# Attention in phases of two slots, with two chunk chains and streamed keys

## The chip, the cores and the metric

The kernel runs on one core of a Trainium2 chip. The metric is the device time of one execution in microseconds (us). Engines are named as in the profile: PE multiplies matrices (PEld is its weight load), DVE is the vector engine, ACT the scalar engine, POOL GpSimd, SP the queue that issues most DMAs. SBUF is the memory that all of them read; PSUM is what PE writes[...].

## The reference, cut to what matters

The network has a Mamba layer and then attention over 2 images of 4096 positions and 256 channels, 8 heads of 32. The change is in the attention alone:

```python
x = x + _L0_conv_ref(_gn(x), ...)            # Mamba layer, unchanged
x = x + _L1_conv_ref(_gn(x), qkv_w, qkv_b, 8)

def _L1_conv_ref(x, qkv_w, qkv_b, num_heads):
    qkv = jnp.einsum('bchw,oc->bohw', x, qkv_w) + qkv_b[None, :, None, None]
    q, k, v = ...                            # (b, 8, 32, 4096) each
    attn_logits = jnp.einsum('bhci,bhcj->bhij', q, k) * scale
    attn_weights = jax.nn.softmax(attn_logits, axis=-1)
    out = jnp.einsum('bhij,bhcj->bhci', attn_weights, v)
    return out.reshape(b, c, h, w)
```

## The kernel before

The Mamba stage comes first and takes the span to about 1995 us. Attention works through image 0, then prepares image 1 (projections of q, k and v, each stored to DRAM and loaded again), then works through image 1. A planner orders the Mamba stage; attention is written out by hand, and each engine runs its instructions in that order.

An image is 2 groups of 4 heads by 8 query tiles of 512 positions, so 16 tiles. Each tile runs over 32 slots, and a slot is 128 keys for 512 queries and 4 heads. A slot needs four logits products on PE (L1162, 128 x 512 each, one PSUM bank each), the exponential on ACT (L1175), four values products (L1199, one per head, accumulated in the bank po), and the sum of the exponentials over all keys, which is the denominator of the softmax.

A slot has two halves, of two heads and so two banks. The six banks of the tile s hold three halves, and a phase is three halves: `sizes` and PHASES (L1144 to L1146) give 20 phases of three halves and two of two in each tile. In `run` (L1314) iteration k has the exponentials of phase k, then the values of phase k-1, then one step of the finishing work of the tile before for each slot (`side.run`), then the logits of phase k+1. In a phase of three halves the values of one slot are whole, 512 columns, and those of another half are 256 columns (`width`, L1193).

The denominators are summed on two engines. The exponentials of heads 0 and 1 go to a buffer `chunk`, which holds four slots side by side; when it is full DVE sums it with one TENSOR_REDUCE into the first place of the next of two buffers (L1184, ten times a tile), and `place` (L1178) says where a slot goes. Heads 2 and 3 go to a tile e. POOL adds both to acc_p (L1239), but in the 15 slots of SHARED it adds one head (L1237), and DVE adds the other to acc_2 in PSUM (L1236). `finish` (L1241) copies po, adds the partial sums (L1249, L1250), sums over the 128 rows on PE with a matrix of ones (L1257), takes reciprocals, multiplies (POOL, L1267), adds bias and residual and stores. `end` (L1276) does it for the last tile.

Keys of a group stay in SBUF: `load_keys` (L1104) loads eight tiles of 1 MB, in two DMAs each, once per group, during the last query tile of the group before.

Of the kernel before, what the change touches and what calls it, by code (L numbers as in the profile page):

```python
# [11 lines left out]
F32 = mybir.dt.float32  # L12
# [17 lines left out]
def group_norm_scales(nc, small, psum_tile, stats, gmat, eps_t, out):  # L30
# [9 lines left out]
    yield  # L40
    ps = psum_tile()
    for k in range(KC):
        nc.tensor.matmul(ps[:, k : k + 1], lhsT=gmat, rhs=mv[k][:, 0:1], start=True, stop=True)
    for k in range(KC):
        nc.vector.tensor_copy(out[k][:, 0:1], ps[:, k : k + 1])

# [5 lines left out]
    yield 4  # L52
    ps = psum_tile()
    for k in range(KC):
        nc.tensor.matmul(ps[:, k : k + 1], lhsT=gmat, rhs=e[k][:, 1:2], start=True, stop=True)
    yield
# [5 lines left out]
class Slots:  # L62
# [10 lines left out]
    def run(self):  # L73
        for entry in list(self.waiting):
            if entry[0] <= self.now:
                try:
                    entry[0] = self.now + (next(entry[1]) or 1)
                except StopIteration:
                    self.waiting.remove(entry)
        self.now += 1  # L80

# [887 lines left out]
def attention(ctx, tc, stats, consts, w, outs, scratch, range_t):  # L969
# [14 lines left out]
    SCALE = 1.0 / math.sqrt(D)  # L984

    p2 = ctx.enter_context(tc.tile_pool(name="l1p2", bufs=2))
    wp = ctx.enter_context(tc.tile_pool(name="l1w", bufs=1))
    ps_s = ctx.enter_context(tc.tile_pool(name="l1pss", bufs=3, space=PSUM))
# [10 lines left out]
    kp = ctx.enter_context(tc.tile_pool(name="l1k", bufs=NT))  # L999
    ep = ctx.enter_context(tc.tile_pool(name="l1e", bufs=5))  # L1000
    ec = ctx.enter_context(tc.tile_pool(name="l1c", bufs=2))
    p1 = ctx.enter_context(tc.tile_pool(name="l1p1", bufs=1))
    p3 = ctx.enter_context(tc.tile_pool(name="l1p3", bufs=2))
    kq = ctx.enter_context(tc.tile_pool(name="l1kq", bufs=1))
# [4 lines left out]
    def s_tile():  # L1009
        return ps_s.tile([P, 2, T], F32, name="s", tag="s")  # L1010

    def chunk():

        return ec.tile([P, 2, 2, T, 2], F32, name="chunk")

    FIRST = 3
    xn = {}  # L1020

    def load_x(t):
# [7 lines left out]
        else:  # L1030
            xn[t] = ep.tile([P, KC, T], F32, name="e")
# [8 lines left out]
    def project(t, i):  # L1040


        pm = s_tile()
        for m in range(KC):
            for c in range(KC):
                nc.tensor.matmul(  # L1046
# [6 lines left out]
        halves = chunk().rearrange("p q h t k -> p q (h t k)").rearrange("p q (m t) -> p q m t", t=T)  # L1053
        for m in range(KC):
            bias = b_qkv[:, i * KC + m : i * KC + m + 1]
            nc.scalar.activation(halves[:, 0, m, :].bitcast(F32R), pm[:, m, :], AF.Identity, bias=bias)
            nc.vector.scalar_tensor_tensor(
                halves[:, 1, m, :].bitcast(F32R), pm[:, m, :], bias, halves[:, 0, m, :], ALU.add, ALU.subtract
            )
            nc.sync.dma_start(scratch.qk[KG + m, i, t].rearrange("s c h t -> (c h) s t"), halves[:, :, m, :])  # L1060

    def project_values(t):
        pm = s_tile()
        flat = pm.rearrange("p a t -> p (a t)")
        for j in range(T // P):
            for c in range(KC):
                nc.tensor.matmul(
# [6 lines left out]
        nc.scalar.copy(v[:, bass.ts(t, T // P), :].rearrange("p s c -> p (s c)"), flat)  # L1074

    def prepare(image):

        for t in range(NT):
# [15 lines left out]
            if 0 < t <= FIRST:  # L1094
                image.load_keys(0, t - 1)
        for t in range(FIRST, NT):
            image.load_keys(0, t)

    def image(b):
# [4 lines left out]
        def load_keys(g, t, queue=nc.sync):  # L1104


            k = keys[g, t] = (kq if g and t == 0 else kp).tile([P, 4, T], F32R, name="k")
            load_stack(queue, k, scratch.qk[b * KG + g, 1, t], 1)
# [7 lines left out]
        def load_prepared():  # L1116
# [6 lines left out]
            load_keys(0, 0, nc.scalar)  # L1123
            load_values(0, 0, nc.scalar)
            for t in range(1, NT):
                load_keys(0, t)
                load_values(0, t)
# [16 lines left out]
        sizes = [3] * ((2 * NC - 4) // 3) + [2, 2]  # L1144
        bounds = [0, *itertools.accumulate(sizes * (KG * NT))]
        PHASES = [range(*ends) for ends in zip(bounds, bounds[1:])]  # L1146
        SHARED = [c for c in range(8, NC) if c % 8 in (0, 2, 4, 5, 6)]
        todo = {}
        tiles = {}

        def logits(s, half):
            if s >= S:
                return
            i, c = divmod(s, NC)
            kt, kj = divmod(c * P, T)
            if half == 0:
                todo[s] = Slot()
                todo[s].s, todo[s].e = [], []
            ps = s_tile()
            for j in range(2):  # L1160
                h = 2 * half + j
                nc.tensor.matmul(  # L1162
                    ps[:, j, :], lhsT=keys[i // NT, kt][:, h, kj : kj + P], rhs=queries[i][:, h, :], start=True, stop=True
                )
            todo[s].s.append(ps)

        def exponentials(s, half):
            if half == 0 and s % NC < NC - 1:
                k = place(s % NC)
                first = s % NC == 0 or k == 1 and s % NC > 1  # L1170
                todo[s].chunk = (todo.pop("chunk", None) or chunk()) if first else todo[s - 1].chunk
                e = todo[s].chunk[:, k // 2, :, :, k % 2]
            else:
                e = ep.tile([P, 2, T], F32, name="e")
            nc.scalar.activation(e, todo[s].s[half], AF.Exp, scale=SCALE)  # L1175
            todo[s].e.append(e)

        def place(c):  # L1178

            return c if c < 4 else 1 + (c - 4) % 3  # L1180

        def sum_chunk(s, out):
            terms = todo[s].chunk.rearrange("p q h t k -> p (h t) q k")
            nc.vector.tensor_reduce(out, terms, AX.XY, ALU.add)  # L1184

        def values(first, end):

            u = first
            while u < end:
                s, half = divmod(u, 2)  # L1190
                i, c = divmod(s, NC)
                g = i // NT
                width = 2 if half == 0 and u + 1 < end else 1  # L1193
                cols = slice(half * T // 2, (half + width) * T // 2)
                u += width
                if c == 0 and half == 0:
# [363 lines left out]
```

## Time and profile before

| what | us |
|---|---|
| median of 3 runs (lowest, highest) | 4287.68 (4287.12, 4287.88) |
| profiled execution, its time | 4289.86 |
| its span, first to last instruction | 4288.1 |
| PE, DVE, ACT, POOL busy in the span | 4119.0, 3855.6, 3729.2, 3751.9 |
| logits products L1162, 4096 of them, busy | 1155.0 |
| values products L1199, busy (into chunk rows, into e rows) | 1057.0, 1020.5 |
| exponentials L1175, to chunk and to e, mean of one | 1.126, 1.028 |
| chunk sums L1184 on DVE, mean of one | 4.409 |
| POOL additions L1239 and L1237, mean of one | 2.432, 1.297 |

The mean granted clock of PE is 0.984 over the span and 1.00 in attention. "Busy" is the time in which an engine executes at least one instruction; products overlap, so a busy PE is not a PE at its peak. A group's row has its line, engine and operation, the tiles it writes and reads, shapes and count, then busy time and the mean of one in ns, then the idle time before it and what ended that. The chain of waits follows the program back from its last instruction, at each step to what released it.

### The profile page before, as it was taken

Reading aid. Unit: us, or ns where it says so; the run is one execution under the profiler, and the core shown is the slowest. Engines: PE = TensorE matmul, PEld = TensorE weight load, DVE = VectorE, ACT = ScalarE, POOL = GpSimd, SP = SyncE. Lnnn points to the kernel's source line nnn. Section 1 sums busy time; section 2 is a strip of 40 time slices with the busy share of each in tenths; the row PEclk is TensorE's granted clock in tenths of the full one; section 3 lists DMA queues with packets and bytes.
Section 4 is the critical chain, followed back from the end, with each engine's and each line's share of the span. In section 5 each row is a group of like instructions: output and inputs, shape, how many; then the busy total and the mean of one; then the engine's idle time right before and its main releaser. Section 6 shows DMA issues by size and latency. Waiting matters only on the chain.

```text
span 4288.1 us, 58982 instructions
## 1 busy us (share of the span) xinstructions
PE 4119.0 (96%) x21176; PEld 1802.7 (42%) x21176; DVE 3855.6 (90%) x3304; ACT 3729.2 (87%) x4983; POOL 3751.9 (87%) x1913
## 2 busy tenths in 40 slices
PE   6799999999999999988999999999999999999998
PEld 2233333333333343333444444444454444444443
DVE  6899999999999999994988989899849889898998
ACT  5789898999788888874999999999859999999997
POOL 3999999999899999994888988889728989888897
PEclk8899999999999999999999999999999999999999
DMA  6334333344444444447101040110181110401100
GB/s 212 105 114 130 113 113 126 129 133 133 150 144 163 154 141 142 142 167 168 34 24 28 18 106 18 28 30 21 40 262 46 40 28 18 106 18 28 30 21 9
DMA packets 172302, 389.58 MB, mean 91 GB/s; under 512 B 23392, under 2 KB 49760, under 8 KB 163808
## 3 DMA queue, kind: packets, MB, share of 16 engines
q1 hardware_dynamic: 171120, 383.37, 29.4%
q8 instruction: 168, 2.75, 0.3%
q10 hardware_dynamic: 880, 2.36, 0.3%
q14 instruction: 134, 1.10, 0.1%
HBM read 292.33 MB, written 93.32 MB: 90 GB/s over the span
## 4 chain that ended last, share of the span: by engine, by line
PE 82%; DVE 10%; ACT 3%; issue 2%; DMA 1%; POOL 1%; SPq 0%; DVEq 0%; POOLq 0%; ACTq 0%
PE s L1162 25%; PE po L1199 24%; PE mm L448 16%; DVE h L869 6%; PE y L901 4%; PE mm L688 4%; PE bn L448 2%; PE mm L647 2%; DVE bn L860 1%; PE s L1046 1%; PE y L899 1%; PE mm L684 1%; PE sums_ps L1257 1%; ACT da L853 1%; ACT L248 1%
## 5 line engine op out<-in xcount | busy, mean ns | idle before, releaser
L1184 DVE TENSOR_REDUCE chunk<-chunk 128x1024 f32<-128x4096 f32 x288 | 1269.9, 4409 | 169.5 <-ACT chunk L1175 168.2
L1239 POOL TENSOR_TENSOR acc_p<-acc_p,e 128x1024 f32<-128x1024 f32 x479 | 1165.1, 2432 | 121.2 <-ACT e L1175 96.6
L875 POOL TENSOR_TENSOR h<-h,c 128x1024 f32<-128x1024 f32 x512 | 1204.5, 2378 | 33.1 <-issue 15.7
L1162 PE MATMUL s<-q,k 128*128 128x512 f32 x4096 | 1155.0, 415 | 7.3 <-ACT chunk L1175 3.1
L1175 ACT ACTIVATE e<-s 128x1024 f32<-128x1024 f32 x1056 | 1081.8, 1028 | 91.4 <-PE s L1162 58.9
L1175 ACT ACTIVATE chunk<-s 128x1024 f32<-128x1024 f32 x992 | 1117.3, 1126 | 49.3 <-PE s L1162 22.5
L1199 PE MATMUL po<-chunk,v 128*32 128x512 f32 (+1 forms) x5248 | 1057.0, 521 | 0.0
L1199 PE MATMUL po<-e,v 128*32 128x512 f32 (+1 forms) x5504 | 1020.5, 500 | 4.2 <-ACT e L1175 4.2
L1162 PEld LDWEIGHTS s<-q,k 128*128 128x128 f32 x4096 | 713.9, 188 | 624.7 <-ACT e L1175 233.9
L853 ACT ACTIVATE da<-dt_rep,neg_a 128x512 f32<-128x512 f32 x1024 | 695.6, 702 | 107.9 <-DVE h L869 103.7
L1237 POOL TENSOR_TENSOR acc_p<-acc_p,e 128x512 f32<-128x512 f32 x480 | 622.3, 1297 | 95.5 <-ACT e L1175 65.7
L869 DVE TENSOR_TENSOR_SCAN h<-da,state,dbu 128x512 f32<-128x512 f32 x512 | 650.1, 1272 | 14.6 <-PE y L901 7.4
L869 DVE TENSOR_TENSOR_SCAN h<-da,state,bn 128x512 f32<-128x512 f32 x512 | 645.6, 1261 | 11.1 <-PE y L901 5.0
L864 POOL TENSOR_TENSOR dbu<-dtu_rep,b 128x1024 f32<-128x1024 f32 x176 | 418.0, 2375 | 18.8 <-issue 9.1
L448 PE MATMUL bn<-proj,pick 112*128 112x512 f32 x512 | 341.9, 669 | 89.1 <-DVE h L869 86.2
L248 ACT ACT_TABLE_LOAD x312 | 400.3, 1283 | 6.2 <-PEq L1550 0.7
L1199 PEld LDWEIGHTS po<-e,v 128*32 128x32 f32 x5504 | 251.6, 109 | 272.1 <-issue 105.3
L860 DVE TENSOR_TENSOR bn<-dtu_rep,bn 128x512 f32<-128x512 f32 x512 | 345.4, 677 | 18.0 <-PE bn L448 8.0
L1199 PEld LDWEIGHTS po<-chunk,v 128*32 128x32 f32 x5248 | 240.2, 108 | 251.2 <-issue 251.2
L1236 DVE TENSOR_TENSOR acc<-acc,e 128x512 f32<-128x512 f32 x448 | 309.5, 691 | 17.4 <-DVE acc L1236 0.5
L901 PE MATMUL y<-h,sum 128*32 128x512 f32 x2048 | 299.3, 613 | 6.9 <-POOL h L875 6.8
L448 PE MATMUL mm<-yn,w_in 128*128 128x512 f32 x512 | 255.2, 623 | 7.9 <-ACT yn L538 3.8
(163 smaller groups left out, 4182.9 us busy)
## 6 DMA issues: line engine op xcount, KB each, us to landing
dt_rep<-dt_dram SPq DMA_DIRECT2D x128, 512.0 KB, 5.0
dtu_rep<-dtu_dram SPq DMA_DIRECT2D x128, 512.0 KB, 5.3
k<-qk_dram SPq DMA_DIRECT2D x62, 512.0 KB, 7.6
q<-qk_dram SPq DMA_DIRECT2D x124, 256.0 KB, 4.8
b<-bc_dram SPq DMA_DIRECT2D x64, 256.0 KB, 3.1
c<-bc_dram SPq DMA_DIRECT2D x64, 256.0 KB, 3.8
dt_dram<-dt SPq DMA_DIRECT2D x64, 256.0 KB, 2.3
dtu_dram<-lw SPq DMA_DIRECT2D x64, 256.0 KB, 3.6
```

Of the source, the lines that this page charges most:

```text
L248: self.nc.scalar.preload_act_table_set(self.TABLES[task.table])
L448: nc.tensor.matmul(out, lhsT=lhsT, rhs=rhs, start=(i == 0), stop=(i == len(pairs) - 1))
L853: nc.scalar.activation(da[j].tile, dt.tile[:, j, :], AF.Exp, scale=scale)
L869: nc.vector.tensor_tensor_scan(h.tile[:, j, :], da[j].tile, dbu, initial, ALU.mult, ALU.add)
L875: nc.gpsimd.tensor_tensor(h.tile, h.tile, rows_c.tile.unsqueeze(1).to_broadcast([P, 2, T]), ALU.mult)
L901: nc.tensor.matmul(y.tile[j * PQ : (j + 1) * PQ, :], lhsT=sum4, rhs=pair[j // 2].h.tile[:, j % 2, :], start=False, stop=(qd == NQ - 1),)
L1162: nc.tensor.matmul(ps[:, j, :], lhsT=keys[i // NT, kt][:, h, kj : kj + P], rhs=queries[i][:, h, :], start=True, stop=True)
L1175: nc.scalar.activation(e, todo[s].s[half], AF.Exp, scale=SCALE)
L1184: nc.vector.tensor_reduce(out, terms, AX.XY, ALU.add)
L1199: nc.tensor.matmul(tiles[i].po[h * D : (h + 1) * D, cols], lhsT=v[:, c, g * P + h * D : g * P + (h + 1) * D], rhs=todo[s].e[h // 2][:, h % ...
L1237: nc.gpsimd.tensor_add(acc_p[:, 1, :], acc_p[:, 1, :], eb[:, 1, :])
L1239: nc.gpsimd.tensor_add(acc_p, acc_p, eb)
```

## The change

A phase becomes two whole slots, and six banks serve eight logits products: the banks of pair `single` are used twice. Heads 2 and 3 of the first slot go there first; each is taken out by an exponential of its own (two instructions of 512 columns), and then heads 0 and 1 of the second slot go into the same banks and are taken out by one of 1024 columns. All four land in the tile e of the phase, 2048 columns wide, of which there are three. Heads 0 and 1 of the first slot and heads 2 and 3 of the second go to chunks, in two chains x and y with three buffers between them. Since the six banks are now one tile, the class `Banks` writes out by hand which instruction waits for which, bank by bank.

POOL adds the whole e in phases 1 to 3 of a tile, and three quarters of it from phase 4 on; DVE adds the remaining head to acc_2. The e of phase 0 is added together with that of phase 1. `finish` gets one more addition on DVE and one on POOL. Values are always whole. Keys have five buffers and are loaded again for every query tile, one key tile every two phases. `group_norm_scales` makes two copies on ACT instead of DVE; `load_x`, `project` and `project_values` take their banks and buffers from the new tiles.

```diff
-    ps_s = ctx.enter_context(tc.tile_pool(name="l1pss", bufs=3, space=PSUM))
+    ps_s = ctx.enter_context(tc.tile_pool(name="l1pss", bufs=1, space=PSUM))
-    kp = ctx.enter_context(tc.tile_pool(name="l1k", bufs=NT))
-    ep = ctx.enter_context(tc.tile_pool(name="l1e", bufs=5))
-    ec = ctx.enter_context(tc.tile_pool(name="l1c", bufs=2))
+    kp = ctx.enter_context(tc.tile_pool(name="l1k", bufs=KEYS))
+    ep = ctx.enter_context(tc.tile_pool(name="l1e", bufs=3))
+    chunks = [wp.tile([P, 2, 2, T, 2], F32, name=f"chunk{n}") for n in range(3)]
+    banks = ps_s.tile([P, 6, T], F32, name="s")
+    log = Banks(tc, banks, "s_")
+    def s_banks(k):
+        return [2 * ((k + n) % 3) for n in range(3)]
...
+        def load_keys(n, queue=nc.sync):
+            if n < KG * NT * NT:
+                k = keys[n] = kp.tile([P, 4, T], F32R, name="k")
+                load_stack(queue, k, scratch.qk[b * KG + n // (NT * NT), 1, n % NT], 1)
...
+        def phase_logits(k):
+            if k >= K:
                 return
+            single, first, second = s_banks(k)
+            places = [(0, 2 + h, single + h) for h in range(2)]
+            places += [(0, h, first + h) for h in range(2)]
+            places += [(1, 2 + h, second + h) for h in range(2)]
+            places += [(1, h, single + h) for h in range(2)]
+            for n, (late, h, bank) in enumerate(places):
+                if n == 6:
+                    e = phases[k] = ep.tile([P, 4, T], F32, name="e")
+                    for j in range(2):
+                        exponential(e[:, j, :], single + j, 1)
+                i, c = divmod(2 * k + late, NC)
+                kt, kj = divmod(c * P, T)
+                mm = nc.tensor.matmul(
+                    banks[:, bank, :],
...
+                log.note(mm, "pe", [bank], True)
+        def exponential(e, bank, n):
+            ps = banks[:, bank, :] if n == 1 else banks[:, bank : bank + n, :]
+            done = nc.scalar.activation(e, ps, AF.Exp, scale=SCALE)
+            log.note(done, "act", range(bank, bank + n), False)
+        def exponentials(k):
+            single, first, second = s_banks(k)
+            e = phases.pop(k)
+            i, n = divmod(k, NC // 2)
+            if n == 0:
+                if "next" not in tiles:
+                    tiles["next"] = chunks[:]
+                tiles["x"], tiles["y"], tiles["free"] = tiles["next"]
+            for late, pair in enumerate((first, second)):
...
+                exponential(terms, pair, 2)
...
+                done = 1 if late and n == 1 else 3
+                if n == NC // 2 - 1:
+                    tiles[i].last[late] = buf
...
+                        sum_chunk(buf, 1 if late else 3, tiles[i].acc[:, late].rearrange("p h t -> p (h t)"))
+                elif at == done:
+                    out = tiles[way] = tiles["free"]
+                    tiles["free"] = buf
+                    sum_chunk(buf, done, out.rearrange("p q h t k -> p q (h t) k")[:, 0, :, 0])
+            if n == NC // 2 - 1:
+                tiles["next"] = [tiles["free"], tiles["x"], tiles["y"]]
+            exponential(e[:, 2:4, :], single, 2)
+            add_up(k, e)
...
+        def values(k):
+            for s in (2 * k, 2 * k + 1):
...
+        def add_up(k, e):
...
+            if n == 0:
+                tile_.acc_p = p3.tile([P, 4, T], F32, name="acc_p")
+                tile_.e = e
+            elif n == 1:
+                nc.gpsimd.tensor_add(tile_.acc_p, tile_.e, e)
+            elif n < 4:
+                nc.gpsimd.tensor_add(tile_.acc_p, tile_.acc_p, e)
+            else:
...
+                    nc.vector.tensor_add(tile_.acc_2, tile_.acc_2, e[:, 0, :])
+                nc.gpsimd.tensor_add(tile_.acc_p[:, 1:4, :], tile_.acc_p[:, 1:4, :], e[:, 1:4, :])
...
-            nc.vector.tensor_add(acc[:, 2, :], d.acc_2, d.acc_p[:, 0, :])
-            nc.vector.tensor_add(acc[:, 0:2, :], acc[:, 0:2, :], todo[i * NC + NC - 1].e[0])
+            yield 2
+            nc.vector.tensor_add(acc[:, 1], acc[:, 1], d.last[1][:, 1, :, :, 0])
+            nc.vector.tensor_add(acc[:, 1, 0, :], acc[:, 1, 0, :], d.acc_2)
+            nc.gpsimd.tensor_add(acc[:, 0], acc[:, 0], d.acc_p[:, 2:4, :])
+            yield
+            nc.vector.tensor_add(acc[:, 1], acc[:, 1], d.acc_p[:, 0:2, :])
             yield 3
...
+                if k < K and (k + 1) % (T // P // 2) == 0:
+                    load_keys(2 * k * P // T + KEYS)
                 phase_logits(k + 1)
```

In the changed file the exponential is L1208, the logits L1197, the values L1262, the chunk sum L1253, the POOL additions L1282, L1284 and L1291, and the new addition of `finish` on POOL L1306.

## The prediction

> **What bounds the kernel now.** I read four views, in this order: the chain of waits over the whole span, the busy time of each engine in a stretch inside attention, the chain inside one query tile, and ScalarE's timeline.
>
> ```profile
> PE 82%; DVE 10%; ACT 3%; issue 2%; DMA 1%; POOL 1%; SPq 0%; DVEq 0%; POOLq 0%; ACTq 0%
> ...
> 2200.00:3000.00 800.00, 799.67 (x5565) 375.36 (x5558) 722.54 (x424) 749.32 (x755) 705.90 (x378) 1.00 0.15 36
> ```
>
> The second row is 2200 to 3000 us: PE, PEld, DVE, ACT, POOL busy, then the granted clock (1.00), DMA share and GB/s. PE is full, but ACT (94%), DVE (90%) and POOL (88%) have little room: a change that gives PE less to do will soon meet them. Attention starts at 1995 us. Copies of po (L1247) come every 67.85 us, once per query tile; there are 32 tiles, so 2171 us of the span are this period. The chain around the end of a tile (start, length, what):
>
> ```profile
> 2540.06 1.60 PE s L1162 x6
> 2541.66 1.52 PE po L1199 x13
> 2543.18 1.12 PE s L1162 x4
> 2544.30 1.53 PE po L1199 x13
> 2545.83 1.12 PE s L1162 x4
> 2546.95 1.04 PE po L1199 x6
> 2548.00 1.60 PE s L1162 x6
> 2549.60 1.00 PE po L1199 x8
> ...
> 2557.16 0.86 PE sums_ps L1257 x8
> ```
>
> Only PE is on it. A phase of three halves is 1.60 for six logits products and 1.52 for the values of one and a half slots: 3.12. A tile has 20 of these and two short phases of one slot, whose logits are the 1.12 rows and whose values the 1.04 and 1.00 rows: logits 20 x 1.60 + 2 x 1.12 = 34.24, values 20 x 1.52 + 2.04 = 32.44, sums 0.86, together 67.54; 0.31 of waits at the boundary makes 67.85. ScalarE in the same stretch:
>
> ```profile
> 2502.14 1.09 ACT L1175 ACTIVATE chunk<-s 128x1024 f32<-128x1024 f32 x1
> 2503.42 1.03 ACT L1175 ACTIVATE e<-s 128x1024 f32<-128x1024 f32 x1 [0.18 <-PE s L1162]
> 2504.34 1.15 ACT L1175 ACTIVATE chunk<-s 128x1024 f32<-128x1024 f32 x1
> 2505.34 1.03 ACT L1175 ACTIVATE e<-s 128x1024 f32<-128x1024 f32 x1
> ```
>
> An exponential of e is followed 0.90 after its start, one of chunk 0.98 to 1.00: they overlap by about 0.1. ACT needs 1.90 per slot of PE's 2.08.
>
> **The change, part by part.** A new phase is two slots: eight logits, five exponentials (S0, S1 of one bank each, E1, E2 of two banks into chunks, E3 of two banks into e), values of two whole slots.
>
> *PE's own work.* Logits: 1.12 for four and 1.60 for six give 0.24 each, so eight take 2.08. Values: 1.52 plus another half. Single records start their passes 0.43 apart, and a half slot is one such step, so 1.95; from the one-slot runs, 1.00 to 1.04, plus 0.86 I get 1.86 to 1.90. I take 1.94, the pass starts being the nearest row. Sum 4.02 for two slots, where before two cost 2 x 66.68 / 32 = 4.17. Over 16 phases 64.3 instead of 66.68: **2.4 us less per tile**, because there are 16 turns from logits to values and back where there were 22[...]. The 40 values products per tile that go (168 to 128) are in this sum already; their weight loads lay beside other products.
>
> *The two products that wait.* The seventh and eighth logits of a phase go into the banks of the first and second, after S0 and S1. This loop PE-ACT-ACT-PE lies inside one phase, and no row before has it. From single records: the first product of a group ends 0.50 after its weight load; ACT starts 0.096 later where a semaphore instruction stands before it (191 starved cases; 0.036 without one, 463 cases), and S0 has one, since it also waits for its e buffer from POOL. S1 follows S0 and needs the duration of a 128x512 exponential that reads PSUM with immediates:
>
> ```profile
> L604 ACT ACTIVATE lw<-mm 128x512 f32<-128x512 f32 x64 | 38.1, 595 | 0.2
> L601 ACT ACTIVATE mm<-mm 128x512 f32<-128x512 f32 x64 | 37.2, 582 | 2.0
> ```
>
> 0.597 long, next start 0.485 later. PE loads weights 0.053 after ACT's end (five stalls). So the eighth weight load starts at 0.50 + 0.096 + 0.485 + 0.597 + 0.053 = 1.73. Undisturbed, the seventh product starts at 0.103 + 6 x 0.234 = 1.51 and hides a weight load that starts up to 0.13 later, 1.64. **0.09 is lost in every phase**, 1.4 per tile. Bounds: 0 (S0 after 0.036, spacing 0.475) and 0.2 (both waits of S0 seen one after the other). S0's end, 1.24, is early enough for the seventh. [...] ACT's total is then 2 x 0.98 + 0.90 + 2 x 0.485 = 3.83 of 4.11: not the bound itself.
>
> *POOL.* Sizes become 2048 for n = 1 to 3 and 1536 for n = 4 to 15; n = 0 adds nothing.
>
> ```profile
> L1230 POOL TENSOR_TENSOR acc_p<-e 128x1024 f32<-128x1024 f32 x12 | 32.0, 2667 | 19.6 <-ACT e L1175 19.6
> L1239 POOL TENSOR_TENSOR acc_p<-acc_p,e 128x1024 f32<-128x1024 f32 x178 | 433.4, 2435 | 41.6 <-ACT e L1175 32.2
> L1237 POOL TENSOR_TENSOR acc_p<-acc_p,e 128x512 f32<-128x512 f32 x176 | 228.0, 1295 | 33.0 <-ACT e L1175 21.9
> ```
>
> 1.14 per 512 elements and 0.16 fixed: 3.57 and 4.71, plus 0.08 between; the first, of two e buffers, twice L1230, 5.17. With the new add of 1024 (L1306) and po x r: 5.2 + 2 x 4.8 + 12 x 3.65 + 2.5 + 1.4 = 62.5 of 68 us. That would fit if it were even, but phase 0's e is held until phase 1's add ends, and the ring is three deep: S0 of phase 3 needs it. From E3 of phase 1: 0.14 + 5.17 + 0.06 = 5.37, where S0 is due one phase and 0.15 after, 4.26. **PE loses 1.1 per tile** (0.6 if this add runs at L1239's rate). The adds behind it stay 0.1 to 1 inside their dates.
>
> *DVE.* Chunk sums stay at ten sets of 4.41 per tile (nine whole, two half). acc_2 goes from 15 terms to 12, -1.9; the finish gains a 1024 add, +1.2: 93% of the new tile. In mid-tile a freed buffer is wanted two to three phases later, cover enough. At the tile's end the first slot's buffer goes straight to the second chain: its sum starts with E1 of phase 15 done and takes 4.41, E2 of the next phase would start 4.0 after that end. ACT is 0.5 late, PE **0.25**. po's copy stands behind this sum and a half one and just makes it before the next values.
>
> *Keys streamed.* 62 key transfers become some 500: 1 MB per two phases, 1 MB / 8.2 us = 128 GB/s. A tile with that load exists before: 2505 to 2540 us shows 132 GB/s, and its period is 67.85 like the others. Each is issued eight phases (33 us) ahead and lands in 7.6, so their place on SP behind stores that wait for DVE costs nothing; behind a key load that waits for PE stand q, res and out, all wanted later still. In the second image's preparation DMA is full (share 0.97, 325 GB/s in 3130 to 3170) and two more key tiles go in before its end: 2 MB / 325 GB/s = 6 us at most, fewer after it; I take +4. The last tile's sum has 23 products instead of 15, two more rounds of four: +1.5. The two copies that group_norm_scales moves from DVE to ACT are 128x1, 0.2 each, once, beside four table loads of 1.28 that stop PE there anyway: nothing.
>
> **Sum.** Tile: 16 x (4.02 + 0.09) + 0.86 + 1.1 + 0.25 = 67.97, against 67.85: 0.12 x 32 = +4. With +5.5 outside the tiles the profiled execution's 4289.86 (span 4288.1 and 1.8 around it) becomes 4299; it stands 2.2 above the median of the runs shown, so **4297 us**. The gain of 76 us, and the 10 of old waits, are paid back by three new ones of 46, 35 and 8.
>
> **Rivals.** *Faster:* the eighth product isn't late and POOL's first add runs at 4.7: 64.3 + 0.86 + 0.25 + 0.6 = 66.0, 1.85 x 32 = 59 less, so 4234 with the 5.5. For it: 0.09 is a difference of sums near 1.7, and POOL's adds in place are shorter. Against: all twelve additions behind L1230's row took 2.66 to 2.67, and no exponential of this size is shorter than 0.58. *Slower:* the loop S0, S1, eighth product is longer than I put it. Place: PE's weight load before the last product of each phase; price 16 x 32 x the excess; from a loss of 0.09 per phase on, the kernel is slower by more than can be mistaken, and at 0.19 (S0 0.1 later) it is 51 more, 4348. For it: up to three semaphores on S0, and a queue that keeps its order, so that every delay moves S1 and E1 too. Against: ACT's starts scatter little before. *The change doesn't do what it says:* a wait that isn't meant, between banks of the single PSUM tile, or a key that comes late, would put logits behind ACT phase by phase: at 4.4 per phase 0.29 x 512 = 148 more, 4445. The built order shows the waits bank by bank, so I give it little.
>
> **How the numbers follow.** Level case 0.52: a loop loss of 0.06 to 0.13 and a POOL loss of 0.6 to 1.4 make 4265 to 4327; the bound of what a measurement can tell, 0.2% or 8.6 us, divides it into 0.10 faster, 0.18 same, 0.24 slower. Faster rival 0.20, slower rival 0.24, unmeant wait 0.04. Together faster 0.30, same 0.18, slower 0.52. The range, 4248 to 4340, takes in the level case and leaves out the far ends of the rivals.
>
> **What would show it.** Periods of po's copy of 68 us; eight logits at 2.17 and values at 1.94 in the chain; ScalarE's 128x512 rows as steps of the chain; one PE wait of about a microsecond per tile released by POOL's 128x2048 add. Wrong if PE's logits take 2.08 with no wait on e (then faster), or if the chain runs through ACT for a whole phase (then slower).

## The result, and the profile after

The changed kernel takes 4340.78 us (median of 4 runs, 4338.25 to 4342.14), the kernel before 4287.78 in the same comparison: a ratio of 1.0119, with an interval of 1.0106 to 1.0132. It is slower, which the prediction had as the likeliest outcome, but by 53 us where 9 were forecast. The median is 0.8 us above the upper end of the range, 4340, less than its runs differ among themselves.

Where the time came from is read from the copies of po, which stand at L1300 now (L1247 before). The profiled executions are compared by their spans, 4288.1 and 4338.3 us:

| stretch | before, us | after, us | difference | predicted |
|---|---|---|---|---|
| start to the first logits of attention | 1995.45 | 2008.10 | +12.65 | 0 |
| first logits to the first copy of po | 80.23 | 84.84 | +4.6 | +0.1 |
| 28 regular tiles, each | 67.85 | 68.82 | 28 x 0.97 = +27.2 | 28 x 0.12 = +3.4 |
| the tile before the preparation of the second image | 72.75 | 74.11 | +1.4 | +0.1 |
| the step across the preparation | 154.92 | 161.86 | +6.9 | +4.1 |
| last copy to the end | 84.8 | 82.4 | -2.4 | +1.6 |

The differences add up to the 50.2 within rounding. Two entries carry the miss: the tile, and the start of attention, where I had put nothing.

Now the views that were shown of before. First the chain of waits over the whole span of the changed kernel, by engine, and the busy time of the engines in the same stretch inside attention (PE, PEld, DVE, ACT, POOL, then clock, DMA share, GB/s):

```profile
PE 73%; DVE 12%; ACT 5%; POOL 4%; DMA 3%; issue 3%; SPq 0%; POOLq 0%; DVEq 0%; ACTq 0%
...
2200.00:3000.00 800.00, 793.95 (x4556) 353.34 (x4554) 775.20 (x406) 744.80 (x931) 717.75 (x199) 1.00 0.65 147
```

PE has lost 9 points of the chain; DVE, ACT, POOL and DMA have taken most of them. DVE is busy for 97% of the stretch, where the prediction's sum made 93%: something that was not in that sum keeps it busy. The chain around the end of a tile (start, length, what):

```profile
2489.34 1.91 PE po L1262 x11
2491.25 2.16 PE s L1197 x8
...
2503.48 0.69 PE s L1197 x2
...
2504.20 1.02 ACT e L1208
...
2509.14 4.64 POOL acc_p L1282
...
2513.80 0.61 ACT e L1208
...
2517.35 0.88 PE sums_ps L1313 x3
...
2518.27 1.05 PE sums_ps L1313 x4
```

In mid-tile the phase is what was predicted: 1.91 for the values (1.94 forecast), 2.16 to 2.17 for the logits (2.17), 4.08 together. The eighth product does wait for its exponential. PE's weight loads for the logits of one phase show it (in square brackets the idle time before, and what ended it):

```profile
2531.46 1.47 PEld L1197 LDWEIGHTS s<-q,k 128*128 128x128 f32 x7 [0.85 <-ACT chunk L1208]
2533.19 0.19 PEld L1197 LDWEIGHTS s<-q,k 128*128 128x128 f32 x1 [0.26 <-ACT e L1208]
```

The eighth load starts 1.73 after the first, as the prediction had worked out. At the tile's end PE loses time at three places: the logits begun at 2503.48 take 3.25 instead of 2.17, those of two phases later end 0.56 late (at 2515.45 instead of 2514.89), and the sums take 1.97 instead of 0.88. Sixteen phases of 4.08 and 0.88 for the sums are 66.16; the tile takes 68.82, so the boundary costs **2.66 us**, where the prediction had 1.35. What the engines wait for there, in the view of waits over twelve tiles (total, times, longest):

```profile
ACT chunk L1208 <- DVE acc_sb L1253: 14.1, 12, 1.2
PEld sums_ps L1313 <- DVE acc_sb L1308: 10.3, 11, 0.9
PEld sums_ps L1313 <- POOL acc_sb L1306: 8.7, 12, 0.7
ACT e L1208 <- POOL acc_p L1282: 7.6, 12, 0.6
```

Three waits: an exponential for a chunk buffer that DVE still reads (1.17 per tile; 0.5 was forecast), the sums' matmuls for two late additions (not forecast; in the tile shown POOL's ends at 2517.13, before the last values do, so that only DVE's is on the chain), and the first exponential of a phase for POOL (0.63, the lower of the prediction's two sizes: the addition of 2x2048 took 4.63, not 5.17). Why DVE is late stands in the timelines of DVE and POOL at that place (start, length):

```profile
2510.39 4.46 DVE L1304 TENSOR_TENSOR acc_sb<-acc_sb,chunk 128x1024 f32<-128x1024 f32 x1
2514.89 0.69 DVE L1305 TENSOR_TENSOR acc_sb<-acc_sb,acc 128x512 f32<-128x512 f32 x1
```

```profile
2509.14 4.63 POOL L1282 TENSOR_TENSOR acc_p<-e 128x2048 f32<-128x2048 f32 x1 [5.61 <-PE s L1197]
2513.70 3.43 POOL L1306 TENSOR_TENSOR acc_sb<-acc_sb,acc_p 128x1024 f32<-128x1024 f32 x1
```

An addition of 1024 took 1.22 on DVE before, in `finish` behind the copy of po (L1250), with POOL idle as it began. Here it takes 4.46. POOL's addition ends at 2513.77, and DVE's 1.08 after that: as if it had stood until then. POOL's next, begun at 2513.70, takes 3.43 where the trace of before had 2.43 for 1024 elements. The second addition of DVE, L1308, takes 2.52 on average for the same size. The two engines seem to work in turn. That is the theory tested below: **a DVE instruction with two inputs in SBUF and an addition of POOL take turns.** L1305, with one input in PSUM (acc_2), keeps its 0.69 while POOL's L1306 runs. The rivals are that the additions only stand in a bad place, or that SBUF is crowded by the streamed keys.

### The profile page after: what moved, and what is told of

Same layout as the page of the kernel before. It is cut to its first block, busy times and chain, and to the rows that moved or that the text cites. A ratio compares the mean times of both kernels' runs of the same rounds, so it can differ in the third digit from the quotient of the medians.

```text
span 4338.3 us, 53353 instructions
## 1 busy us (share of the span) xinstructions
PE 4134.0 (95%) x18632; PEld 1759.0 (41%) x18632; DVE 4016.2 (93%) x3267; ACT 3744.6 (86%) x5497; POOL 3810.9 (88%) x1432
## 3 DMA queue, kind: packets, MB, share of 16 engines
q14 instruction: 128, 1.04, 0.1%
## 4 chain that ended last, share of the span: by engine, by line
PE 73%; DVE 12%; ACT 5%; POOL 4%; DMA 3%; issue 3%; SPq 0%; POOLq 0%; DVEq 0%; ACTq 0%
PE s L1197 22%; PE po L1262 20%; PE mm L477 14%; DVE h L898 6%; PE mm L717 4%; PE y L930 4%; POOL acc_p L1282 3%; PE bn L477 2%; PE mm L676 2%; DVE chunk L1253 1%; PE sums_ps L1313 1%; DVE bn L889 1%; ACT e L1208 1%; ACT da L882 1%; ACT L277 1%
## 5 line engine op out<-in xcount | busy, mean ns | idle before, releaser
L1291 POOL TENSOR_TENSOR acc_p<-acc_p,e 128x1536 f32<-128x1536 f32 x383 | 1357.9, 3545 | 52.1 <-ACT e L1208 28.5
L1253 DVE TENSOR_REDUCE chunk<-chunk 128x1024 f32<-128x4096 f32 (+1 forms) x288 | 1198.8, 4162 | 112.2 <-ACT chunk L1208 111.7
L1197 PE MATMUL s<-q,k 128*128 128x512 f32 x4096 | 1179.7, 424 | 34.6 <-issue 14.2
L1208 ACT ACTIVATE e<-s 128x512 f32<-128x512 f32 (+1 forms) x1536 | 1094.2, 751 | 126.9 <-PE s L1197 73.0
L1208 ACT ACTIVATE chunk<-s 128x1024 f32<-128x1024 f32 x1024 | 1095.6, 1138 | 38.1 <-DVE acc_sb L1253 33.7
L1197 PEld LDWEIGHTS s<-q,k 128*128 128x128 f32 x4096 | 728.2, 189 | 757.7 <-ACT chunk L1208 395.7
L1262 PE MATMUL po<-chunk,v 128*32 128x512 f32 x4096 | 1022.6, 635 | 0.0
L1262 PE MATMUL po<-e,v 128*32 128x512 f32 x4096 | 1010.7, 599 | 0.0
L1282 POOL TENSOR_TENSOR acc_p<-e 128x2048 f32<-128x2048 f32 x32 | 148.1, 4629 | 265.5 <-PE s L1197 162.3
L1262 PEld LDWEIGHTS po<-chunk,v 128*32 128x32 f32 x4096 | 193.9, 109 | 435.3 <-issue 427.2
L889 DVE TENSOR_TENSOR bn<-dtu_rep,bn 128x512 f32<-128x512 f32 x512 | 347.0, 680 | 17.3 <-DMA dtu_rep<-dtu_dram 9.4
L1284 POOL TENSOR_TENSOR acc_p<-acc_p,e 128x2048 f32<-128x2048 f32 x64 | 324.7, 5073 | 12.6 <-ACT e L1208 10.0
L1290 DVE TENSOR_TENSOR acc<-acc,e 128x512 f32<-128x512 f32 x351 | 241.3, 688 | 7.0
```

The lines of the kernel that those rows point to most:

```text
L1197: mm = nc.tensor.matmul(banks[:, bank, :], lhsT=keys[i * NT + kt][:, h, kj : kj + P], rhs=queries[i][:, h, :], start=True, stop=True,)
L1208: done = nc.scalar.activation(e, ps, AF.Exp, scale=SCALE)
L1262: nc.tensor.matmul(tiles[i].po[h * D : (h + 1) * D, :], lhsT=v[:, c, g * P + h * D : g * P + (h + 1) * D], rhs=todo[s].e[h], start=(c == 0 ...
L1291: nc.gpsimd.tensor_add(tile_.acc_p[:, 1:4, :], tile_.acc_p[:, 1:4, :], e[:, 1:4, :])
```

## The experiments

"Tile" is the median period of po's copies. Each ratio is against runs of the kernel before beside it; the changed kernel stands at 1.0119.

| run | time, us | ratio | interval | tile, us |
|---|---|---|---|---|
| e1 early additions | 4304.21 | 1.0034 | 1.0022 to 1.0047 | 67.60 |
| e2 fourth chunk buffer | 4304.01 | 1.0035 | 1.0019 to 1.0051 | 67.71 |
| e3 place of the buffers | 4328.38 | 1.0095 | 1.0066 to 1.0124 | 68.85 |
| e4 keys not streamed | 4338.91 | 1.0119 | 1.0090 to 1.0149 | 68.81 |
| e5 fourth e buffer | 4334.96 | 1.0103 | 1.0082 to 1.0123 | 68.83 |
| e6 later matmul of the norm | 4342.92 | 1.0121 | 1.0101 to 1.0141 | 68.83 |
| e7 merged exponentials | 4478.8 (one run) | | | 73.23 |
| e8 together | 4247.78 | 0.9900 | 0.9883 to 0.9916 | 66.44 |
| e9 second input from PSUM | 4288.57 | 1.0002 | 0.9992 to 1.0012 | 67.08 |
| e10 three key tiles | 4334.57 | 1.0104 | 1.0072 to 1.0135 | 68.82 |
| e11 e1 and e2 together | 4300.69 | 1.0030 | 1.0020 to 1.0039 | 67.59 |
| e12 e8 and the norm from PSUM | 4250.94 | 0.9911 | 0.9893 to 0.9929 | 66.45 |

### e1: the additions ahead of POOL's

```diff
             nc.sync.dma_start(res, x[g * P : (g + 1) * P, cols])
-            yield 2
             nc.vector.tensor_add(acc[:, 1], acc[:, 1], d.last[1][:, 1, :, :, 0])
...
             nc.vector.tensor_add(acc[:, 1], acc[:, 1], d.acc_p[:, 0:2, :])
-            yield 3
+            yield 5
```

> The two DVE additions and the POOL addition of finish move from phase 1 to phase 0, where POOL has nothing to do; the sums stay where they are. Theory (the end of a tile): L1304 takes 4.46 us instead of 1.2 because POOL is adding at the same time, and the products of sums_ps wait for it, 1.1 us per tile. Then L1304 falls to 1.2 to 1.5, the wait goes, the tile is 67.7 us instead of 68.82 and the kernel about 4307. Rival (DVE is simply full, 97 per cent busy): DVE has the same work, so the wait moves to another phase, the tile stays within 0.3 us of 68.82 and the kernel above 4330.

The time fell by 36 us. The groups of instructions from 2200 to 3000 us show the first of the same two additions (its line is one lower; count, busy, mean ns):

```profile
L1303 DVE TENSOR_TENSOR acc_sb<-acc_sb,chunk 128x1024 f32<-128x1024 f32 x12 | 16.6, 1382 | 0.0
```

4.46 and 2.52 have become 1.38 and, for the second, 1.23. The edit moves the additions too, so it does not yet tell the turns from the place; e9 does.

### e9: same place, second input from PSUM

```diff
-            nc.vector.tensor_add(acc[:, 1], acc[:, 1], d.last[1][:, 1, :, :, 0])
+            at = b * KG * NT + i
+            twice = d.acc_2.unsqueeze(1).to_broadcast([P, 2, T])
+            nc.vector.tensor_reduce(range_t[:, 1, at : at + 1], d.last[1][:, 1, 0, 0:2, 0], AX.X, ALU.max)
+            nc.vector.tensor_add(acc[:, 1], acc[:, 1], twice)
...
-            nc.vector.tensor_add(acc[:, 1], acc[:, 1], d.acc_p[:, 0:2, :])
+            nc.vector.tensor_reduce(range_t[:, 1, at : at + 1], d.acc_p[:, 0, 0:2], AX.X, ALU.max)
+            nc.vector.tensor_add(acc[:, 1], acc[:, 1], twice)
```

> Same place, same size, but the second input of VectorE's two 1024-element adds at a tile's end comes from PSUM (acc_2, twice) instead of SBUF; an instruction of two elements with one SBUF input keeps each add's wait and what it releases. Left out: the terms of these two adds, so the sums of two heads, and the output, differ. Theory (a VectorE instruction with two inputs in SBUF waits for the end of the GpSimd instruction that runs, and the next GpSimd instruction for it): the first add falls from 4.46 to about 1.3 us, the second from 2.52 to about 1.25, GpSimd's add of 1024 from 3.40 to about 2.4, the tile from 68.82 to between 67.4 and 68.2 us, the kernel to about 4298 to 4322. Rival (the adds are long because SBUF is busy with transfers and with all engines, or because they are counted from an early start): they stay above 3 us, and the tile stays at 68.8.

DVE and POOL in one tile's end of this run:

```profile
2566.04 1.21 DVE L1307 TENSOR_TENSOR acc_sb<-acc_sb,acc 128x1024 f32<-128x1024 f32 x1
```

```profile
2564.73 4.64 POOL L1282 TENSOR_TENSOR acc_p<-e 128x2048 f32<-128x2048 f32 x1 [4.95 <-PE s L1197]
2569.33 2.38 POOL L1309 TENSOR_TENSOR acc_sb<-acc_sb,acc_p 128x1024 f32<-128x1024 f32 x1
```

At the same place, inside POOL's addition (2564.73 to 2569.37), the same size of addition takes 1.21 (the second 1.22), and POOL's next is back at 2.38. The rival falls: neither the place nor the traffic had changed (150 GB/s from 2200 to 3000 us, 147 in the changed kernel). The tile is 67.08, 1.74 shorter, more than I expected; the long additions had cost two thirds of the boundary's 2.66. ACT's waits are now 0.47 per tile for DVE and 0.61 for POOL, and there is none for the two additions before the sums. DVE catches up within the tile again: in the twelve tiles it waits 37.9 us for ACT before its chunk sums of four slots, where in the changed kernel that wait was 0.0. So the long additions also made DVE release a chunk buffer late at the next tile's start.

Both halves of the theory stand in the traces: beside an addition of POOL, an addition of 1024 on DVE takes 4.46 with two inputs in SBUF, and POOL's next 3.43; with one input in PSUM they take 1.21 and 2.38. The prediction did not look for either.

### e2, e5, e11: one wait behind another

A fourth chunk buffer (with three key tiles in place of five, to pay for it in SBUF):

```diff
-    KEYS = 5
+    KEYS = 3
...
-    chunks = [wp.tile([P, 2, 2, T, 2], F32, name=f"chunk{n}") for n in range(3)]
+    chunks = [wp.tile([P, 2, 2, T, 2], F32, name=f"chunk{n}") for n in range(4)]
...
-                tiles["next"] = [tiles["free"], tiles["x"], tiles["y"]]
+                tiles["next"] = [tiles["free"], tiles["spare"], tiles["x"], tiles["y"]]
```

> A fourth chunk buffer (and three key buffers instead of five, to make room), so that the second chain of a tile doesn't begin in the buffer that DVE is still summing. Theory (the end of a tile): the ACT wait of 1.2 us for L1253 goes, PE gets back about 1.0 us per tile: tile 67.8, kernel about 4309. Rival (DVE is full): the wait is found again at the next use of a buffer, tile above 68.5, kernel above 4330. With three key buffers a late key would show as PE waiting for a DMA; none is expected.

The theory held: the wait of ACT for DVE is gone, and the tile is 67.71 (67.8 expected), though DVE's first addition still takes 4.45. Some 6 of its 37 us are not the buffer's: the step across the preparation falls to 156.13 with the three key tiles, as in e10. A fourth buffer for the exponentials that POOL adds:

```diff
-    KEYS = 5
+    KEYS = 4
...
-    ep = ctx.enter_context(tc.tile_pool(name="l1e", bufs=3))
+    ep = ctx.enter_context(tc.tile_pool(name="l1e", bufs=4))
```

> The ring of exponentials that GpSimd and VectorE add gets a fourth buffer (four key tiles instead of five pay for it in SBUF). In the changed kernel the first exponential of a phase waits about 0.6 us a tile for GpSimd's add of 2x2048, which opens the tile's sum. Theory (this wait is one of three that follow each other at a tile's edge): it goes, the tile falls from 68.82 to about 68.3 us, the kernel to about 4322 us; the long VectorE adds (4.46 us) stay. Rival (the three waits overlap, and GpSimd's is in the shadow of VectorE's): the tile stays at 68.8 and the time above 4335 us.

The rival held for the tile: 68.83. The wait of ACT for POOL has gone, and the wait of the sums has grown by nearly as much, as a row of its view of waits shows:

```profile
PEld sums_ps L1313 <- POOL acc_sb L1306: 14.9, 12, 1.3
```

The sums now wait 1.24 instead of 0.73 per tile for POOL's addition of 1024, which takes 3.39 behind DVE's (2.40 in e9). Most of the 6 us that the kernel gained lie in the step across the preparation (157.50 instead of 161.86), which is e10's matter. Then the two edits that each gave over a microsecond, together:

> The early adds of VectorE and the fourth chunk buffer together, with three key tiles, and without the fourth exponential buffer. Theory (the two waits that they take away are separate): the tile is 68.82 - 1.20 - 1.03 = 66.6 us, as with everything together, and the kernel takes about 4266 us (the early key load is missing). Rival (they take away the same wait twice): the tile stays near 67.6 us and the time above 4290 us.

Here my theory fell: 67.59, the tile of e1 alone. Its rival had the number, but not quite the reason. It was not the same wait twice; a third took its place, as the waits show:

```profile
ACT e L1208 <- POOL acc_p L1282: 15.3, 12, 1.3
```

This was 0.63 per tile in the changed kernel, 0.28 in e1, and is 1.28 here. DVE's early addition now goes first and holds up POOL's (L1282 takes 5.53 instead of 4.63), and with three e buffers ACT waits for it longer. In e8 below POOL's addition takes as long, 5.52, and with four e buffers there is no such wait. So the three waits of a boundary stand one behind another, and what one edit gains depends on the others.

### e7: the loop inside a phase

```diff
-                    for j in range(2):
-                        exponential(e[:, j, :], single + j, 1)
+                    exponential(e[:, 0:2, :], single, 2)
```

> The two exponentials of 512 columns of a phase are merged into one of 1024 columns; nothing else is changed. Theory of the prediction (a phase is logits, whose eighth product waits for the first exponential, and then values; no engine's throughput is the limit): the eighth product waits for the longer exponential, logits grow from 2.17 to about 2.6 us, a phase from 4.08 to 4.5, a tile to about 75.5 us, the kernel to 4530 to 4560 us, though ScalarE is busy for less of the time. Rival (a phase is limited by ScalarE's throughput): a phase gets shorter by one instruction's fixed cost, about 0.1 us, a tile by about 1.5, the kernel to about 4297 us.

The phase is what the prediction's loop gives. The chain through two phases:

```profile
2508.86 1.04 ACT e L1207
...
2513.35 1.04 ACT e L1207
2514.43 0.73 PE s L1196 x2
```

The merged exponential starts every 4.49 us (2508.86, 2513.35), and two products of logits stand behind it. The rival, which made the phase shorter, falls. PE's weight loads of one phase, as they were shown of the changed kernel:

```profile
2512.53 1.24 PEld L1196 LDWEIGHTS s<-q,k 128*128 128x128 f32 x6 [0.86 <-ACT chunk L1207]
2514.43 0.30 PEld L1196 LDWEIGHTS s<-q,k 128*128 128x128 f32 x2 [0.66 <-ACT e L1207]
```

The loads that wait start 1.90 after the first, where it was 1.73, and two products come after instead of one, a step of 0.23: together the 0.40 by which the phase grew. So the reason given beforehand, a longer exponential, was not quite right: one of 1.04 ends no later after its start than two of 0.597 begun 0.495 apart (1.09), as they are in the changed kernel, but it can start only when both banks are full. The tile is 73.23, not 75.5: 16 x 4.48 and 0.88 are 72.6, so the boundary costs 0.7 instead of 2.66. I had added the longer phases to unchanged waits. That longer phases give DVE and POOL time to catch up fits their busy shares, 90% instead of 97% and 84% instead of 90%.

### e3, e6, e12: the start of attention

In the changed kernel the first load of keys is issued at 1995 us, when the stage before has left its SBUF place, and the first logits stand behind that transfer. The chain of the changed kernel there:

```profile
1995.15 9.45 DMA k<-qk_dram
2004.60 3.50 issue
2008.10 2.06 PE s L1197 x4
```

In e3 the chunk buffers get a pool of their own, allocated after the others:

```diff
-    chunks = [wp.tile([P, 2, 2, T, 2], F32, name=f"chunk{n}") for n in range(3)]
+    cp = ctx.enter_context(tc.tile_pool(name="l1c", bufs=1))
+    chunks = [cp.tile([P, 2, 2, T, 2], F32, name=f"chunk{n}") for n in range(3)]
```

> The chunks are allocated after the keys, in a pool of their own, so that the first key tile has another place in SBUF. Theory (place): the first key load waits until 1994.7 because its place is one that the Mamba stage frees last; then the first logits start near 1996 instead of 2008.1, the tile period stays 68.82 and the kernel loses 12 us to about 4328. Rival (the longer SP and ACT queues of the new loads delay it): the start stays near 2008 and the kernel at 4340.

First logits at 1995.79, as before the change (1995.45); the time is 12.4 us less, with a tile of 68.85. The 12.65 of the table are an accident of which buffer lies where.

The other 4.6 us lie between the first logits and the first copy. PE stands 5.3 us there before the second matmul of the group norm. DVE and POOL just ahead of it in the changed kernel:

```profile
2018.31 3.37 DVE L49 TENSOR_TENSOR gn_e<-gn_mv,gn_sc 128x1 f32<-128x1 f32 x1
...
2021.91 4.34 DVE L51 TENSOR_TENSOR gn_e<-gn_e,gn_mv 128x1 f32<-128x1 f32 x1
```

```profile
2017.05 4.62 POOL L1282 TENSOR_TENSOR acc_p<-e 128x2048 f32<-128x2048 f32 x1 [52.32 <-ACT e L1208]
2021.75 4.49 POOL L1284 TENSOR_TENSOR acc_p<-acc_p,e 128x2048 f32<-128x2048 f32 x1
```

These are the turns at their barest: a subtraction and an addition of *one element* per partition take 3.37 and 4.34 us, and end at 2021.68 and 2026.25, within 0.02 of the end of POOL's additions. First I only put the matmul later (`yield 4` for the second `yield 2` of `group_norm_scales`):

> The second matmul of the group norm is put two phases later, so that VectorE, which is behind in its chunk sums there, has its input ready. Theory (TensorE stands 5.3 us at this matmul in the first tile of each image, as the trace shows for the first): the stall goes, the first tile's copy of the values comes 4 to 5 us earlier, the kernel takes about 4336 us, the tile stays at 68.82. Rival (VectorE is the bound there, and TensorE would wait for it a phase later anyway): the first copy moves by less than 1 us, and the time is 4340 us.

The rival held. From the first logits to the first copy it took 84.25 instead of 84.84, and PE still stands 5.5 us at this matmul. In e12, on top of everything in e8, the operations take an input from PSUM instead:

```diff
-        nc.vector.tensor_sub(e[k][:, 0:1], mv[k][:, 0:1], out[k][:, 0:1])
-        nc.vector.tensor_mul(e[k][:, 1:2], e[k][:, 0:1], e[k][:, 0:1])
-        nc.vector.tensor_add(e[k][:, 1:2], e[k][:, 1:2], mv[k][:, 1:2])
+        d = ps[:, 2 + k : 3 + k]
+        nc.vector.tensor_sub(d, mv[k][:, 0:1], ps[:, k : k + 1])
+        nc.vector.tensor_sub(e[k][:, 0:1], mv[k][:, 0:1], ps[:, k : k + 1])
+        nc.vector.tensor_mul(d, e[k][:, 0:1], d)
+        nc.vector.tensor_add(e[k][:, 1:2], d, mv[k][:, 1:2])
```

> All changes together, as in e8, and one more: VectorE's operations of the group norm take one of their two inputs from PSUM (four operations of one element instead of three), so that none has two inputs in SBUF. Theory (these operations of one element take 3.4 to 4.6 us because they wait for the end of GpSimd's add, and the group norm's matmul, the chunk sums behind them and the exponentials wait in turn): each takes about 0.2 us, the time from the first logits to the first copy of the values falls from 81.7 us to 77.5 to 80, the kernel from 4247.8 to about 4245. Rival (they are late for another reason, such as the chunk sum before them): they stay at 3 us or more, or PE's first tile is no shorter, and the time stays within 1 us of e8's.

Half of each. The operations take 0.15 to 0.16 us each, beside an addition of POOL that runs from 2007.68 to 2012.31:

```profile
2008.93 0.15 DVE L50 TENSOR_TENSOR gn_ps<-gn_mv,gn_ps 128x1 f32<-128x1 f32 x1
```

So an input from PSUM ends the turns a second time, and yet nothing is gained: 81.86 us from the first logits to the first copy, 81.69 in e8. PE now stands 5.12 us at logits that wait for an exponential behind ACT's table loads for the norm (1.28 each, on the chain in both).

About 3 of the 4.6 us had already come back in e3, whose edit doesn't touch the norm: 81.83 from the first logits to the first copy. With the keys early, only the first of the norm's operations there meets an addition of POOL (3.03 us), the second matmul has its input in time, and PE stands 5.13 us behind the same table loads. So the turns in the norm can account for some 3 of the 4.6 us at most; the rest stays open.

### e4, e10: the keys

e4 loads only the first five key tiles of each image and reads them over and over, so its output is a different one:

> Keys are loaded for the first five key tiles of each image alone and used again in place of all others, so the output is another one; PE, ACT, DVE and POOL have the same instructions. Theory (the end of a tile): the tile stays 68.82 within 0.1, and the kernel within 8 us of 4340. Rival (streaming): 147 GB/s beside the engines slows their reads and writes of SBUF; then the tile falls by 0.5 us or more, to the 67.85 of before at the most, and the kernel by 16 to 31 us.

68.81 per tile, and 161.89 across the preparation, with 25 GB/s of transfers from 2200 to 3000 us instead of 147: the transfers cost nothing where they stream, as the prediction had it. The rival of a crowded SBUF falls too: DVE's first addition takes 4.46 here as well. e10 has three key tiles instead of five and is otherwise the changed kernel:

> Three key tiles instead of five, nothing else: fewer keys are loaded ahead, in the second image's preparation too. Theory (the preparation of the second image is 6 us longer than before because two more key tiles are loaded at its end, where the transfers are full): the step across it falls from 161.9 to about 156.5 us, the tile stays at 68.82, the kernel takes about 4335 us. Rival (the step is long because of the chunk buffers or the exponentials at the turn of the images; the fourth buffers of the two earlier runs shortened it, not the keys): the step stays within 1 us of 161.9 and the time at 4340.

The step across the preparation falls from 161.86 to 155.66. The time falls by 6.2, but its two runs, 4330.9 and 4338.2, lie wide apart; the step is the firmer evidence. Less a tile, it is 86.8 against 87.1 before the change: all of the preparation's 6 us came from the two more key tiles loaded at its end.

### e8: a version that beats both

The edits of e1, e2, e3 and e6, with four e buffers; to make room, `res` has one buffer and the last tile's sum uses a buffer of `acc_sb`.

> All that the earlier runs found put together on the changed kernel: VectorE's adds at the tile's end are issued early, ahead of GpSimd's; a fourth chunk buffer; a fourth exponential buffer; three key tiles; the second group norm matmul two phases later; the chunk buffers in a pool of their own behind the keys, so that the first keys load earlier. Theory (the waits at the tile's edge are separate and add up, 0.56 + 1.08 + 1.1 us, and what is left is sixteen phases of 4.08 and the matmuls of the sums): a tile of about 66.5 us and 4235 to 4255 us in all, faster than the kernel before by about 1%. Rival (behind these waits VectorE or TensorE is the bound, and each repair uncovers the same limit): the tile stays near 67.6 as in the two single repairs, and the kernel takes 4280 to 4295 us, the same as before.

4247.78 us, 1.0% less than the kernel before (interval 0.9883 to 0.9916) and 93 less than the changed one. The chain at a tile's end now runs on PE alone, with one step of DVE (the copy of po):

```profile
2540.26 1.63 PE s L1198 x6
2541.89 0.69 DVE po_sb L1301
...
2548.68 2.17 PE s L1198 x8
2550.85 1.91 PE po L1263 x11
2552.76 0.88 PE sums_ps L1313 x8
```

Its tile of 66.44 leaves 0.28 above the 66.16 of PE's own steps. The forecast was right, though its reason, that the waits are separate and add up, was not: e5 and e11 show that they cover one another, and of the runs made only this one, with all the edits, clears them.

## Why the prediction was right, and where it failed

- **The phase: right.** 2.08 + 0.09 + 1.94 = 4.11 was forecast; 2.17 + 1.91 = 4.08 was measured. That the eighth product waits for an exponential of one bank shows in its weight load, 1.73 after the first as worked out, and in e7, where a later exponential made the phase longer. The rows (0.597 and 0.485) were near: in the changed kernel these exponentials take 0.597 and start 0.495 apart. The faster rival, in which the eighth product is not late, is out (its other half, POOL's first addition at 4.7, came true with 4.63), and so is the unmeant wait. The slower one's number, 4348, lies near the measured time, but its mechanism, a longer phase, is not what happened.
- **Keys streamed: right at no cost (e4).** The preparation was put at +4 and measured +6.0, which was the bound stated beside it; e10 gives the mechanism.
- **The finish on DVE: the step that failed.** "The finish gains a 1024 add, +1.2" priced each addition by a row measured while POOL was idle, and did not ask what POOL would be doing at the new place. The two additions take 4.46 and 2.52, `scalar_tensor_tensor` at the end 2.68 where it took 0.74, POOL's addition of 1024 another 1.0. With DVE so late, its chunk sum releases its buffer late (1.17 instead of 0.5), which costs PE 1.08 where I had 0.25. And the sums' matmuls, for which I had no wait at all, cost PE 1.09.
- **The same step's proof.** e9 takes the turns out of these two additions and leaves the rest. What it then shows is near the boundary as forecast: ACT 0.47 late for DVE (I had 0.5), 0.61 for POOL (see below), and no wait for an addition before the sums. It costs 67.08 - 66.16 = 0.92; I had 1.35. The boundary was out by 2.66 - 1.35 = 1.31, the phases and sums by -0.46; the net 0.85 over some 31 tiles is 26 us of the miss.
- **POOL's first addition: a misread row.** The 5.17 is twice the 2.67 of L1230, less one fixed 0.16. But in the trace of before DVE's last addition runs as L1230 begins, here in one tile; the third line gives the shortest, median and longest of the 32:

```profile
2551.87 1.22 DVE L1250 TENSOR_TENSOR acc_sb<-acc_sb,e 128x1024 f32<-128x1024 f32 x1
2552.68 2.67 POOL L1230 TENSOR_TENSOR acc_p<-e 128x1024 f32<-128x1024 f32 x1 [1.63 <-ACT e L1175]
L1230 POOL TENSOR_TENSOR acc_p<-e x32: 2384/2668/2668, 2001.5 to 4205.3; 128x1024 f32<-128x1024 f32 x32
```

In thirty tiles the two overlap by 0.40 to 0.42 us and L1230 takes 2.66 to 2.67; in the first tile of each image no such addition of DVE's runs beside it, and it takes 2.38 and 2.40. Twice 2.38 less 0.16 is 4.60, and 4.63 was measured; PE loses 0.56 here, not 1.1. So the turns already stood in a row that the prediction shows. Overlooked, it made this term too large and the one on DVE too small.

- **The side came true in part by luck.** With the turns taken out of two additions alone (e9) the kernel is level with the one before, 1.0002, though the start of attention and the preparation still cost some 16 and 7 us in it. The reasons that the prediction gave come to 9 us, hardly more than the 8.6 that it called the bound of what a measurement can tell.
- **The start of attention: not looked at.** I put nothing for the place of the keys in SBUF, and the change cost 12.65 us there (e3). And of the group norm I wrote "nothing", since its copies were short; its other operations, which the change doesn't touch, came beside POOL's additions, which can account for some 3 of the 4.6 us there at most. Together 17.3.
- **The end: +1.5 forecast, -2.4 measured.** No run was made on it; it stays open.

## What to carry to other kernels

Before a VectorE instruction with two inputs in SBUF is put anywhere, look at what GpSimd runs there (here additions in SBUF): price it as GpSimd's remaining time plus its own (3.38 and 1.08 of the 4.46), lengthen GpSimd's next by about the latter (3.43 here, 2.38 in e9), and give it an input in PSUM (1.21, e9) or issue it before GpSimd starts (1.38, e1, where GpSimd's addition behind it took 5.13 instead of 4.63). Where waits follow one another at a boundary, removing one tells little; look at what becomes late next, and repair them together. When buffers are added or resized, look at what was in their place before, and whether the first load of the stage now waits for it.

## What was not expected of the hardware

- A VectorE subtraction of 128x1 took 3.37 us and an addition 4.34 us, ending within 0.02 us of GpSimd's additions of 2048; with one input in PSUM they took 0.15 to 0.16 beside such an addition.
- Each engine waits for the other: GpSimd's addition of 2x2048 took 4.63, and 5.53 where VectorE's addition of 1024 had started first (e11); its addition of 1024 took 3.40, and 2.40 where VectorE's had an input in PSUM (e9).
- VectorE's chunk sums (4.40 in the changed kernel and in e9), which have one input, and its additions into acc_2 in PSUM (0.69 in both) keep their length beside a GpSimd that is busy for 90% and 89% of the time; both are as long in the kernel before (4.41 and 0.69).
